# Four graph layers on one core: the first pairs of the second layer ahead of the first layer's last sums, with checks, constants and turned factors in another order

## The chip, the core and the metric

The kernel runs on one core of a Trainium2 chip. The core has five instruction queues: TensorE (PE, matrix products, with its weight loads as PEld), VectorE (DVE), ScalarE (ACT), GpSimd (POOL) and SyncE (SP, which here only issues loads and stores). Each works through its own instructions in the order in which they were put down; between engines they wait for one another on semaphores. Data lie in SBUF; PE writes to PSUM[...]. The metric is the device time of one execution in microseconds, the median of several runs. A profile of one further execution shows where the time goes.

## The reference

Four layers run over one graph of 4096 nodes with 64 features each. `adj` is a dense 4096 by 4096 matrix of zeros and ones in float32, 64 MB, and every layer needs all of it. After each layer comes `x = layernorm(x + layer(x))`. Cut to what matters:

```python
# layer 0: mean over neighbours
deg = clip(sum(adj, 1) + 1, 1);  h = (adj @ x + x) / deg
z = relu(concat([x, h], 1) @ W + b);  out = z / max(norm(z), 1e-12)
# layers 1 and 3: attention in hyperbolic space, over all pairs (i, j)
left, right = logmap0(x) @ w_l, logmap0(x) @ w_r
a = sigmoid(left[:, None] + right[None, :] + b) * adj
out = proj(expmap(x, einsum('ij,ijd->id', a, logmap(x[:, None], x[None, :]))))
# layer 2: the last 100 neighbours, weights halving from the end of the row
w = mask * where(pos > 0, 0.5 ** (k - pos), 0);  out = w @ (x @ weight) + bias
```

## The kernel before

**Tiles and stages.** The 4096 nodes are cut into four groups of 1024 (`s`), worked through as 3, 2, 1, 0 (`GROUPS`). For a group, the matrix comes in 16 loads of 1 MB (`load`, L706): load `g`, from 15 down to 0, holds blocks `2g+1` and `2g` of 128 source nodes by the group's 1024 target nodes. So each layer takes 64 loads; I count them through, load 0 to 63 in layer 0, so that load `16n + 15 - g` is load `g` of the n-th group. All come through SP, into six buffers (`f_loads`): a load is issued when all readers of the one six before it are done.

**Layer 0** (L1556 to 1613). Each load gets eight products on PE (L1571): the features as a high and a middle part (`first`) and as a low part with a column of ones (`third`), which gives sums and degrees in four PSUM banks of a group (`acc`, six banks in all). DVE checks for each of the 256 parts of the matrix that it holds zeros and ones only (`check`, L869, one instruction of 128x2048). `checked_later` (L712) puts half of the checks of every group into layer 2, where the same part is loaded again; in layer 0 the checks of `g` = 15, 14, 13, 12, 10, 8, 6 and 4 are done. At a group's end ACT copies the four banks to SBUF, and the *row work* of the group follows: `end_0` (L1507: products with the weights at L1519 and L1520, division by the degree, relu, norm), `norm_rows`, and `prepare` (L950), whose second half (`second`, L970) makes the group's factors for the pairs. Four of them are turned (transposed on PE at L1025, copied on ACT at L1029): `hi_lo` and `src`, with which the group enters the pairs as sources, and `lo_hi` and `dst`, with which it enters as targets, and which are needed only when its own 1024 targets have their turn. For the last group of the order much of that runs on POOL instead of DVE (`pooled`). `constants` (L1478) spreads the biases over the partitions and makes the columns of the attention weights.

**Layers 1 and 3** (`attend`, L1118). For each target group, each of 16 loads makes two half steps: six products into a tile `z` of two banks (L1152, 1155, 1158), `sig` and `sq` on ACT (L1170, L1173), `t = max(z, 0) * sig` on DVE (L1176); and for both halves together `t = (sq + c) * t` on DVE (L1179) and eight products into the sum `acc` (L1130), two loads later. `need((layer, 2 * g // WB))` asks for the source group's factors before the first load that uses them: the last group's at the 13th load.

**Layer 2** (`wide_pass`, `narrow_pass`) counts neighbours with products at L1756, takes powers on ACT (L1763) and adds up at L1722 and L1768. `supports` (L1398) makes `x @ weight` of a group from rows: `x_hl` on ACT and POOL (L1403, L1404), turned on PE (L1409), multiplied (L1419).

**Order.** Row work is written as generators that `yield` a number of ticks. `later` puts one into one of two queues; `tick` (L617) is called some times for each load and runs what is due; `need` ticks until something is done. `take` (L677) hands out the PSUM bank for row work (`aux`), and every second time a spare one while there is one; `spare_ends` ticks until none is in use. In layers 0 and 2 the order of PE and ACT is that of the program text (`FIXED`); else the scheduler places instructions. `anchored`, where set, puts row work of PE, ACT and DVE behind the pair work (or checks) that stands before it in the text.

**The border from layer 0 to layer 1.** After its last load the last group's four banks are copied by ACT, `end_0` is queued, and `need((0, s, "rows"))` runs it up to its division, then `spare_ends`. Only then `attention` begins.

## Time and profile before

| what | time |
|---|---|
| median of 3 runs | 1062.61 us (1061.79 to 1067.7) |
| the profiled execution | 1063.81 us |
| its span in the profile | 1062.1 us |
| mean granted PE clock | 0.975 of full |
| layer 0, to the last copy of its sums | 0 to 184.1 us |
| layer 1, first to last target group | 188 to 515 us |
| layer 2 | 515 to 716 us |
| layer 3 and the end | 715 to 1062 us |

The stages are read from the first and last instructions of L1571, L1152 and L1756 in the timeline. The profile's page gives busy time by engine and in 40 slices of 26.6 us; the trace behind it can be asked for the timeline of one engine, for waits, for the chain of work that ended last, and for busy time in chosen stretches. In a timeline row stand the start, the duration, the engine, the line, what is written from what, the count, and in brackets the idle time before it and what ended that.

### The profile page before, as it was taken

Reading aid. Unit: us, or ns where it says so; the run is one execution under the profiler, and the core shown is the slowest. Engines: PE = TensorE matmul, PEld = TensorE weight load, DVE = VectorE, ACT = ScalarE, POOL = GpSimd, SP = SyncE. Lnnn points to the kernel's source line nnn. Section 1 sums busy time; section 2 is a strip of 40 time slices with the busy share of each in tenths; the row PEclk is TensorE's granted clock in tenths of the full one; section 3 lists DMA queues with packets and bytes.
Section 4 is the critical chain, followed back from the end, with each engine's and each line's share of the span. In section 5 each row is a group of like instructions: output and inputs, shape, how many; then the busy total and the mean of one; then the engine's idle time right before and its main releaser. Section 6 shows DMA issues by size and latency. Waiting matters only on the chain.

```text
span 1062.1 us, 13509 instructions
## 1 busy us (share of the span) xinstructions
PE 981.6 (92%) x4760; PEld 401.9 (38%) x4845; DVE 900.2 (85%) x1383; ACT 753.1 (71%) x876; POOL 339.0 (32%) x695
## 2 busy tenths in 40 slices
PE   5998998889999999999999999999899999999991
PEld 2454554333333333333333344543333333333330
DVE  7577877788999999999475579858899999999996
ACT  0013122779989888898667688897898888888870
POOL 0011212480155365365210020104401562573660
PEclk8899999899999999999999999999999999999996
DMA  9999999755665666567589999996465765665600
GB/s 357 359 418 368 394 390 387 300 180 176 238 208 207 220 238 207 189 238 238 204 300 336 371 366 304 327 333 233 143 218 194 243 232 204 242 207 203 234 1 23
DMA packets 38580, 271.62 MB, mean 256 GB/s; under 512 B 4710, under 2 KB 4710, under 8 KB 5734
## 3 DMA queue, kind: packets, MB, share of 16 engines
q1 hardware_dynamic: 37728, 270.03, 69.6%
q8 instruction: 40, 0.66, 0.2%
q10 hardware_dynamic: 774, 0.63, 0.2%
q14 instruction: 38, 0.31, 0.1%
HBM read 269.58 MB, written 1.05 MB: 255 GB/s over the span
## 4 chain that ended last, share of the span: by engine, by line
PE 62%; DVE 21%; ACT 6%; POOL 6%; issue 2%; DMA 2%; ACTq 0%; SPq 0%; POOLq 0%; DVEq 0%
PE acc L1130 16%; PE z L1756 11%; PE z L1155 7%; PE z L1158 7%; PE z L1152 7%; DVE t L1179 6%; DVE t L1176 6%; PE acc L1571 5%; PE z L1768 3%; DVE junk L871 2%; PE z L1722 2%; DMA edges<-in_adj_dram 2%; ACT sq L1173 2%; ACT sq L1763 1%; POOL sq L1535 1%
## 5 line engine op out<-in xcount | busy, mean ns | idle before, releaser
L1176 DVE SCALAR_TENSOR_TENSOR t<-z,sig 128x1024 f32<-128x1024 f32 x256 | 309.1, 1219 | 22.4 <-ACT sq L1173 20.1
L1173 ACT ACTIVATE sq<-z 128x1024 f32<-128x1024 f32 x256 | 255.1, 1022 | 59.1 <-PE z L1158 29.2
L1179 DVE SCALAR_TENSOR_TENSOR t<-sq,t 128x2048 f32<-128x2048 f32 x127 | 293.3, 2309 | 0.3
L1170 ACT ACTIVATE sig<-left_b,right 128x1024 f32<-128x1024 f32 x256 | 286.6, 1149 | 3.6 <-DVE t L1176 3.2
L1130 PE MATMUL acc<-t,xe 128*64 128x512 f32 x1024 | 259.8, 611 | 7.9 <-DVE t L1179 7.0
L1155 PE MATMUL z<-lo_hi,hi_lo 128*128 128x512 f16 x512 | 194.4, 380 | 3.8 <-issue 1.1
L1158 PE MATMUL z<-dst,src 74*128 74x512 f16 x512 | 195.4, 382 | 0.0
L1152 PE MATMUL z<-edges,two_i 128*128 128x512 bf16 x463 | 181.8, 393 | 5.8 <-DVE t L1176 5.8
L1763 ACT ACTIVATE sq<-z 128x512 bf16<-128x512 f32 (+1 forms) x192 | 137.9, 741 | 43.0 <-PE z L1756 41.2
L1130 PEld LDWEIGHTS acc<-t,xe 128*64 128x64 f32 x1024 | 64.2, 137 | 137.2 <-issue 109.8
L871 DVE SCALAR_TENSOR_TENSOR t<-edges 128x2048 bf16<-128x2048 f32 x32 | 73.3, 2300 | 28.7 <-DMA edges<-in_adj_dram 28.5
L1152 PEld LDWEIGHTS <-two_i 128*128 128x128 bf16 x512 | 50.3, 98 | 124.7 <-issue 74.3
L1571 PE MATMUL acc<-edges,first 128*128 128x512 bf16 x241 | 77.9, 400 | 16.8 <-DMA edges<-in_adj_dram 16.3
L1756 PE MATMUL z<-edges,pass_by 128*128 128x512 bf16 x241 | 85.2, 390 | 6.8 <-ACT sq L1763 5.8
L1756 PE MATMUL z<-edges,enter 128*128 128x512 bf16 x248 | 86.3, 388 | 0.4
L871 DVE SCALAR_TENSOR_TENSOR junk<-edges 128x2048 bf16<-128x2048 f32 x32 | 73.1, 2284 | 15.7 <-DMA edges<-in_adj_dram 15.7
L1571 PE MATMUL acc<-edges,third 128*65 128x512 bf16 x256 | 81.1, 398 | 0.8 <-issue 0.2
L1158 PEld LDWEIGHTS <-src 74*128 74x128 f16 x512 | 49.3, 96 | 73.0 <-issue 11.6
L1155 PEld LDWEIGHTS <-hi_lo 128*128 128x128 f16 x512 | 50.4, 98 | 58.3 <-issue 12.8
L1279 POOL TENSOR_TENSOR w_att<-x,u 128x512 f32<-128x512 f32 x6 | 18.1, 3022 | 163.5 <-ACT u L1273 163.5
L1722 PE MATMUL z<-sq,halves 128*128 128x512 bf16 x122 | 45.9, 377 | 0.8 <-ACT sq L1763 0.6
L1535 POOL TENSOR_TENSOR sq<-z 128x512 f32<-128x512 f32 x4 | 10.1, 2524 | 114.2 <-DVE z L1533 94.6
(466 smaller groups left out, 1002.3 us busy)
## 6 DMA issues: line engine op xcount, KB each, us to landing
edges<-in_adj_dram SPq DMA_DIRECT2D x256, 1024.0 KB, 4.9
x<-in_x_dram SPq DMA_DIRECT2D x4, 256.0 KB
out_dram<-x ACTq DMA_DIRECT2D x2, 256.0 KB
out_dram<-x SPq DMA_DIRECT2D x2, 256.0 KB
w_sb<-in_L_gnn_W_dram ACTq DMA_DIRECT2D x1, 32.0 KB, 5.3
w_twice<-in_L_gnn_weight_dram ACTq DMA_DIRECT2D x2, 16.0 KB, 4.6
given<-in_L_gnn_b_dram ACTq DMA_DIRECT2D x1, 0.2 KB
given<-in_L_gnn_bias_dram ACTq DMA_DIRECT2D x1, 0.2 KB
```

The lines of the kernel that those rows point to most:

```text
L871: V.scalar_tensor_tensor(junk, a, 0.0, a, ALU.not_equal, ALU.not_equal, accum_out=odd[:, n : n + 1])
L1130: it = nc.tensor.matmul(acc[h * D : (h + 1) * D, :], xe[:, j, :], t[:, k, h * W : (h + 1) * W], start=j == BLOCKS[0], stop=j == BLOCKS[-1],)
L1152: nc.tensor.matmul(half, two_i, edge[:, at : at + W], start=True, stop=False)
L1155: nc.tensor.matmul(half, hi_lo[:, of], lo_hi[:, to], start=False, stop=False)
L1158: last = nc.tensor.matmul(half, src[:, of], dst[:, to], start=False, stop=True)
L1170: nc.scalar.activation(sig, left_b, AF.Sigmoid, bias=right[:, j : j + 1])
L1173: nc.scalar.activation(sq[:, k], zp, AF.Square, bias=ROOT + OFF, scale=-1.0 / UNIT)
L1176: V.scalar_tensor_tensor(ts[k][:, k], zp, 0.0, sig, ALU.max, ALU.mult)
L1179: V.scalar_tensor_tensor(t, sq, HIGH**2, t, ALU.add, ALU.mult)
L1571: nc.tensor.matmul(accs[h][:m], lhs[:, j, :], edge[:, at : at + W], start=j == BLOCKS[0], stop=j == BLOCKS[-1],)
L1756: nc.tensor.matmul(z[:, h : h + W], lhs, rhs[:, h : h + W], start=j == BLOCKS[0], stop=True, skip_group_check=True,)
L1763: weighed[0] = nc.scalar.activation(w, z[:, :n], AF.Exp, bias=-(OFF_EDGE + CUT) * LN2, scale=-LN2)
```

## The change

1. The checks of `g` = 6 and 4 of groups 3 and 2 move from layer 0 to layer 2.
2. `constants` becomes a generator in the queue, with waits of some ticks between its parts; `att_columns` is cut into the products (`att_products`) and the rest. The first group's `linear` follows behind it in the same queue entry.
3. In layer 0, row work is anchored from the second group on.
4. In layers 1 and 3, group 1 is treated as group 0 in that `lo_hi` and `dst` are turned last, after the group counts as ready (`late`). In layer 1's preparation, group 1 takes its two logarithms as a series on DVE (`half_log_of_ratio`) instead of on ACT.
5. At the end of layer 0 ACT loads the sigmoid's table by an activation of one element; half of the four copies goes to DVE; and `end_0` of the last group is not run there. `attention` queues it, to begin 4 ticks into the pairs, with `attend`'s own bank `acc` as the spare bank until the first products of L1130 need it.
6. `supports` waits 4 ticks instead of 2 for `x_hl` in layer 2.

```diff
             def checked_later(s, g):
-                return g in (0, 1, 2, 3, 5, 7, 9, 11)
+                return g in (0, 1, 2, 3, 5, 7, 9, 11) or (s in GROUPS[:2] and g in (4, 6))
...
-                    by_log = layer == 3 and s != GROUPS[-1]
+                    by_log = s != GROUPS[-1] and (layer == 3 or s == GROUPS[-2])
...
-                    for parts in turns[:2] if pooled else turns:
+                    late = s in GROUPS[2:]
+                    for parts in turns[:2] if late else turns:
                         yield from turn(*parts)
...
                     done.add((layer, s))
-                    if pooled:
+                    if late:
                         for parts in turns[2:]:
                             yield from turn(*parts)
...
                 acc = ps.tile([P, W], F32, name="acc")
+                if layer == 1 and s == GROUPS[0]:
+                    spare.append(lambda dtype, shape: of_bank(acc, dtype, shape))
...
                             if len(lag) == 2:
+                                if spare:
+                                    spare_ends()
                                 add_up(*lag.pop(0), last)
...
-                yield 2
+                yield 4 if place[0] == 2 else 2
...
                     t = aux.tile([P, 2 * D + 3], F32, name="aux")
                     nc.tensor.matmul(t, one_row, given, start=True, stop=True)
+                    yield 4
                     V.tensor_copy(given_b, t)
+                    yield 8
...
-                    return (
-                        curved(c1, "k1", 1e-15**0.5), curved(c3, "k3", 1e-15),
-                        att_columns(att_rows1, "att1"), att_columns(att_rows3, "att3"),
-                    )
+                    made.append(curved(c1, "k1", 1e-15**0.5))
+                    made.append(curved(c3, "k3", 1e-15))
+                    for rows_of, name in ((att_rows1, "att1"), (att_rows3, "att3")):
+                        w = att_products(rows_of)
+                        yield 8
+                        made.append(att_columns(w, name))
+                    yield 4
...
                     for s in GROUPS:
+                        anchored[0] = s != GROUPS[0]
...
-                                curve1, curve3, att1, att3 = constants()
...
-                                later(in_turn((0, s), linear(0, s, w0_sb[:D, :], own_part)))
+                                own_of = linear(0, s, w0_sb[:D, :], own_part)
+                                later(in_turn((0, s), constants(), own_of))
                             tick(4)
                         need((0, s))
+                        curve1, curve3, att1, att3 = made
+                        last = s == GROUPS[-1]
+                        if last:
+                            nc.scalar.activation(turned_on, one_row[:, :1], AF.Sigmoid)
                         tops = []
                         for h in range(2):
                             top = row.tile([P, W], F32, name="sums", bufs=2)
-                            nc.scalar.copy(top, sums[h])
+                            copy = V.tensor_copy if last and h else nc.scalar.copy
+                            copy(top, sums[h])
...
-                            nc.scalar.copy(low, counts[h][: D + 1])
+                            copy(low, counts[h][: D + 1])
                             tops.append((top, low))
-                        later(end_0(s, tops))
-                        if s == GROUPS[-1]:
-                            need((0, s, "rows"))
+                        if not last:
+                            later(end_0(s, tops))
...
                     anchored[0] = n > 0
                     then = GROUPS[n + 1] if n + 1 < NW else None
+                    if n == 0 and layer == 1:
+                        later(end_0(GROUPS[-1], tops), False, 4)
                     sums = attend(layer, s, rates[n], then)
```

`of_bank` is the old `of_third` of layer 2, made general: it gives a PSUM bank the shape that is asked for.

More of the change, by code (lines that the diff above doesn't have):

```diff
@@ L684, in take, with of_bank @@
                 return spare[0](dtype, shape)
+            def of_bank(t, dtype, shape):
+                if dtype == F16:
+                    return t.bitcast(F16)
+                n = int(np.prod(shape[1:]))
+                if len(shape) == 2:
+                    return t[:, :n]
+                names = "abc"[: len(shape) - 1]
+                return t[:, :n].rearrange(
+                    "p (%s) -> p %s" % (" ".join(names), " ".join(names)),
+                    **dict(zip(names, shape[1:])),
+                )
             def spare_ends():
@@ L848, in att_rows, with att_products @@
                 return t
-            def att_columns(rows_of, name):
+            def att_products(rows_of):
                 t = aux.tile([P, 2], F32, name="aux")
@@ L858, in att_columns @@
                     )
+                return t
+            def att_columns(t, name):
                 w = row.tile([P, 2], F32, name="att_w")
@@ L1531, in end_0 @@
                     held.clear()
-                    done.add((0, s, "rows"))
                     V.tensor_scalar(z, z, 0.0, None, ALU.max)
@@ L1553, in end_0 @@
                     )
+                made = []
+                turned_on = keep.tile([1, 1], F32, name="turned_on")
                 with tc.manual_schedule(engines=FIXED):
                     for s in GROUPS:
+                        anchored[0] = s != GROUPS[0]
                         sums = [ps.tile([P, W], F32, name="acc") for _ in range(2)]
@@ L1613, in stream @@
                 spare_ends()
+                anchored[0] = False
             place[0] = 1
@@ L1777, in stream @@
             row_bank = ps.tile([P, W], F32, name="acc")
-            def of_third(dtype, shape):
-                t = row_bank
-                if dtype == F16:
-                    return t.bitcast(F16)
-                n = int(np.prod(shape[1:]))
-                if len(shape) == 2:
-                    return t[:, :n]
-                names = "abc"[: len(shape) - 1]
-                return t[:, :n].rearrange(
-                    "p (%s) -> p %s" % (" ".join(names), " ".join(names)),
-                    **dict(zip(names, shape[1:])),
-                )
             with tc.manual_schedule(engines=FIXED):
-                spare.append(of_third)
+                spare.append(lambda dtype, shape: of_bank(row_bank, dtype, shape))
                 for some in (GROUPS[:2], GROUPS[2:3], GROUPS[3:]):
```

## The prediction

> **What bounds the kernel now.** First I read the page for the engines as a whole: the busy rows and the slices.
>
> ```profile
> PE 981.6 (92%) x4760; PEld 401.9 (38%) x4845; DVE 900.2 (85%) x1383; ACT 753.1 (71%) x876; POOL 339.0 (32%) x695
> ...
> DVE  7577877788999999999475579858899999999996
> ...
> DMA  9999999755665666567589999996465765665600
> ```
>
> The averages hide three regimes. In layer 0 (seven slices) the DMA row is at 9 and DVE is not: the loads decide. In the attention slices DVE is at 9 and DMA at 5 or 6: there each load costs DVE two L1176 and one L1179, 2 x 1.15 + 2.2 = 4.5 us from start to start. The change touches the loads of layer 0, the border to layer 1, one wait in layer 2 and the border to layer 3; the middle of the pairs stays as it is.
>
> Second, does layer 0 load at full speed? I added the trace's DMA packets up to loads of 1 MB and took each load's last packet. Loads 16 to 27 land 2.51 us apart (53.24 to 80.86); that is full speed. Longer gaps stand at loads 8 to 12 (29.31 to 43.34: 14.0 for four), 29 and 31 (3.57 and 4.17), 45 and 47 (3.84 and 4.18), 63 (3.91). The chain of waits has three of them, the last right behind a check of DVE:
>
> ```profile
> 90.30 7.08 DMA edges<-in_adj_dram
> ...
> 133.86 6.91 DMA edges<-in_adj_dram
> ...
> 173.09 2.22 DVE junk L871 x2
> 175.36 5.34 DMA edges<-in_adj_dram
> ```
>
> So buffers come free too late, and SP's own waits say who frees them: checks first (103.6 us), PE second.
>
> ```profile
> SPq L708 <- DVE junk L871: 103.6, 28, 6.3
> SPq L708 <- PE acc L1571: 37.7, 27, 7.5
> ```
>
> Third, the timeline of PE in the first group. PE stands for `given_b`, which DVE copies only behind two checks; load 3 had landed at 15.3, its products start at 24.7, and SP issues load 9, into its buffer, at 28.34.
>
> ```profile
> 16.22 0.49 PE L1481 MATMUL aux<-given,one_row 1*128 1x131 f32 x2
> 21.04 1.01 PE L855 MATMUL aux<-one_row,xw 1*128 1x1 f32 x4 [4.33 <-DVE given_b L1482]
> 22.30 1.01 PE L855 MATMUL aux<-one_row,xw 1*128 1x1 f32 x4 [0.25 <-DVE att_w L860]
> ```
>
> Fourth, the border to layer 1: DVE stands for the last sums, then for POOL, and PE with it.
>
> ```profile
> 185.00 0.18 DVE L1525 RECIPROCAL deg<-aux 128x4 f32<-128x4 f32 x1 [4.70 <-PE aux L1520]
> ...
> 191.64 1.22 DVE L1176 SCALAR_TENSOR_TENSOR t<-z,sig 128x1024 f32<-128x1024 f32 x1 [0.32 <-ACT sq L1173]
> 196.68 0.69 DVE L924 TENSOR_REDUCE n_m<-z 128x8 f32<-128x512 f32 x1 [3.82 <-POOL z L1542]
> ```
>
> Fifth, layer 2, where PE is the bound (9.4 to 9.9 of 10 us busy, but 7.79 from 540 to 550):
>
> ```profile
> 543.76 0.62 PE L1409 MATMUL aux<-ident,x_hl 128*128 128x128 f16 x8 [2.14 <-DVE un L756]
> 544.21 0.61 PE L1756 MATMUL z<-edges,pass_by 128*128 128x512 bf16 x2
> 544.66 0.78 PE L1756 MATMUL z<-edges,enter 128*128 128x512 bf16 x2
> 545.37 1.92 PE L1768 MATMUL z<-sq,halves 128*64 128x512 bf16 x8
> ```
>
> The name in the bracket is only the last signal; DVE's `un` is not read here. POOL's L1404 makes `x_hl` from 540.42 to 543.70.
>
> **The change, part by part.** Sums are made against the profiled run, 1063.81 us (span 1062.1); it lies 1.2 us above the median of the runs, so the forecast is the gain taken off the median.
>
> *Constants in steps.* In the new order PE does three loads between the product for `given` and the first `att` products, and two more before the second. DVE's order up to the fourth check is the same: that check ends at 20.8, so load 9 can be issued then, long before load 8's packets end. Four gaps fall from 14.0 to 10.0: **-4.0**. The small steps of the attention columns only change places among rows of 0.15 us; the parts of `first` for groups 2, 1 and 0 come near 16, 25 and 37, before loads 4, 8 and 12 land (17.8, 29.3, 39).
>
> *Four checks fewer.* They take 4 x 2.29 = 9.2 us from DVE in layer 0. On the path is only load 31, issued at 89.88 when the check begun at 87.52 ended: 4.17 - 2.5 = **-1.7**. Load 29 waits for `g` = 8, which stays behind the norm's row work (80.59): its 1.1 stays. In layer 2 the same 9.2 us fall between 563 and 582, where DVE waits for loads (4.7, 2.3 and 4.4 us idle before the next piece); PE holds such a buffer some 9 us longer than the check would, so nothing. Without that cover: 9.2.
>
> *Anchored order.* In groups 1 and 0 DVE's new order has the checks of `g` = 6 and 4 ahead of two 0.69 us steps and some eight small ones. The gap at load 47 falls from 1.7 to 0.5 over 2.5, that at 63 from 1.4 to 0.1; load 45 still waits for `g` = 8 and loses 0.3: about **-2.4**. Sum for the loads: the last one of layer 0 lands at 179.6 - 8.1 = 171.5, and its products end near 174.6.
>
> *The end of layer 0.* Here DVE is late next. Load 48 lands 6.6 earlier, at 133.4, and DVE has just then ended group 2's row work, so the checks of group 0 begin at 134.0 instead of 140.87; 25 us to `g` = 8 as before (140.87 to 165.88), 2.3 for it, 3.3 for ten small and two large row steps, 4.6 for two checks: 169.5. Behind them now stands group 1's second half: 5.5 us of old steps, the logarithm's 17 new ones at 0.1 to 0.2 (3.2), three to `f` (0.6), then two copies (0.6 each, 0.55 apart): 179.9. What the logarithm takes away is two 0.2 us activations and a 0.36 us wait, so it costs 3 us of DVE. PE's queue holds the sums of the half that DVE copies *ahead* of the first pairs: all pairs stand behind DVE. PE idles 175.4 to 180.0, then 2.1 us of sums and 1.3 of pairs at full clock, 1.1 for `sq`: first L1176 at 184.5. Here a rule bears. The Trainium skill (TensorE: Matmul & The Clock Gate, Part 1) has PE at half clock after an idle window of some 3.4 us and for as long after. The row: after 3.56 us idle at 198.67 pair products ran 0.42 apart, not 0.22. So 3.0 + 2.6 + 1.1: 186.8. But at 543.76 a wait of only 2.14 was enough: L1768's eight took 1.92, not 1.05. I take the cold value, by these rows; both ends stay. Before it was 191.64. The early table load costs nothing: in the old run its 1.28 (at 185.03) lay in ACT's wait for PE too.
>
> *The last group's row work among the pairs.* I compare at the end of the 12th L1179, 261.87 before. From 191.64 that is 70.2 us: 24 x 1.15 + 12 x 2.2 = 54.0 of pairs, 6.2 row work, 10.0 idle (3.82, 2.22, 0.75, 1.57, 1.35, 0.25). After: row work 6.2 - 1.0 (group 1's last steps) + 3.2 (division to norm, once before the pairs) = 8.4; idle 1.5 at the start, 3.0 for POOL's first root (5.3 against two L1176), 1.2 at the variance, 1.4 at the reciprocal, 2.0 at the logarithm's activation: 9.1. So 186.8 + 71.5 = 258.3 cold, 255 or so warm: 3.6 to 6.9, I take **-4.0**. It is half of what the loads gain.
>
> *`supports` two ticks later*: one half step, 2.9 us; PE then arrives at 544.2, POOL is done at 543.70. The wait of 2.14 goes, and with it the slow products: steps from 539.55 to 545.37 and on to 550.12 took 10.6 where 2.9 each plus 0.45 and 0.7 for the turns make 7.0. By the rule above 2.14 us is too short an idle to cool, so -2.1; by the row -3.6. I take **-3.3**. Group 1's `halves` come under 1 us later (L1426 at 551.76 before) and are needed from 555.7 on, group 0's 2.9 later than 576.9, needed near 583.
>
> *Right factors of group 1 last.* In layer 2's last pass each ACT copy of 0.9 lengthened its step by 0.63 (starts 1.99 instead of 1.36 apart); two go: -1.3. In the pairs of layer 3 they meet a DVE that is full from 719 to 732; ACT has room but for the first steps. Bounds 0 and -2.5 (with the chain of group 0 earlier); **-1.2**, near the row.
>
> Sum: -4.0 - 3.3 - 1.2 = **-8.5**: 1055.3 for the profiled run, 1054.1 on the median.
>
> **Rivals.** *The loads' gain comes through whole.* If DVE is done by 175.5 (its pieces in layer 0 are 0.08 apart where independent, 0.2 where not; I took the middle) the pairs start at 180 to 182: 8 + 3.3 + 1.2 = 12.5, 1050. Against it: the new steps are a chain. *The border takes everything.* If DVE is 4 later than 179.9, only 4.5 is left: 1058. For it: the gain in the loads counts for nothing once DVE is last. *Slower: the chain of group 0 comes too late for the 13th load.* Place: POOL's steps among L1179. The Trainium skill (SBUF — State Buffer, Who interferes with whom) says DVE and POOL exclude each other on a shared port for a whole instruction; here POOL steps that began in an L1179 took 2.17 to 2.35 instead of 0.20, seven of them before 250 (14 us of a chain of 65). By the rows' order I count one block less at the first root and one less at the second; by the rule any step that meets an L1179 blocks. Ten more blocks are 20 us: the chain ends near 277 instead of 257, the 13th load waits, and of the border's -4 a +15 is left, less 4.5 from the later layers: 1073. The change loses from four or five more blocks on (8.5 over 2). Against it: two of the covers in the new order are L1176 alone, which reads PSUM.
>
> **How the numbers follow.** Forecast 0.57 (own range 1050 to 1058), whole gain 0.16, border takes all 0.18, slower 0.09. The range 1047 to 1062 leaves out the slower case and the ends of the others. A difference of 0.5% (5.3 us) is what a measurement of this kernel can tell from none: below 1057.3 is faster. The forecast gives 0.53 of its chance to that and the whole gain all of it: 0.69. The border case and a rest of the forecast make 0.22, slower 0.09.
>
> **What would show it.** Load 12 landing near 39 and load 63 near 171 to 173; no wait over 1 us at the `att` products; DVE's copies of the last sums ending near 180 with PE idle before them; the 12th L1179 of layer 1 ending 3 to 7 us earlier; no wait at L1409 near 540. I am wrong if layer 0's loads still show gaps of 4 us at loads 9 and 10, if the 13th load waits for its factors, or if layer 2's loads are issued behind checks.

## The result and the profile after

The changed kernel takes **1050.22 us** (median of 4 runs, 1049.27 to 1051.42) where the kernel before takes 1062.99 (1061.79 to 1067.7): a ratio of 0.9865, 95% interval 0.9833 to 0.9898. The profiled execution took 1051.42 us with a span of 1049.7. On a second chip (the sixth experiment) the ratio was 0.9894, 0.987 to 0.9919, from 1062.87 to 1050.42.

The page of the changed kernel, engines first and then slices:

```profile
PE 977.7 (93%) x4845; PEld 397.9 (38%) x4845; DVE 907.8 (86%) x1401; ACT 751.7 (72%) x873; POOL 322.1 (31%) x695
...
DVE  7486978789999999999488579858999999999996
...
DMA  8999999655665566566599998996465666665600
```

The busy times hardly moved. What moved are the waits. SP's own show that layer 0 now loads better: it waited 10.5 us less for checks and 4.9 less for PE than before (103.6 and 37.7).

```profile
SPq L720 <- DVE junk L886: 93.1, 26, 6.4
SPq L720 <- PE acc L1598: 32.8, 23, 2.4
```

The lines have shifted: a check is L886, the pairs' steps on DVE are L1196 and L1199, the sums of layer 0 L1544 and L1545, the turned products of `supports` L1429. (In some of the experiments they lie a few lines off.) The page counts the checks too: 32 in layer 0 and 32 in layer 2 before, 28 and 36 now. That is 64 in all, one of 128x2048 for each load of 1 MB, and not 256 as the description of the kernel has it.

At the end of layer 0, DVE's timeline shows its two copies, then eight small steps of row work up to 181.2, then nothing until the first pair:

```profile
179.02 0.68 DVE L1636 COPY u<-acc 65x512 f32<-65x512 f32 x1
179.62 0.68 DVE L1628 COPY sums<-acc 128x512 f32<-128x512 f32 x1
...
187.56 1.23 DVE L1196 SCALAR_TENSOR_TENSOR t<-z,sig 128x1024 f32<-128x1024 f32 x1 [6.33 <-ACT sq L1193]
```

PE's timeline tells why. It stood 4.11 us for DVE. The bracket names `own` (L1070), the last reader of the PSUM bank that the sums go to; it ends 0.2 us behind the copies, which stand ahead of it in DVE's order. The products behind the wait run 0.43 us apart, at half clock, until 187.06; from 187.43 on they are 0.22 apart:

```profile
180.63 0.66 PE L1544 MATMUL aux<-sum_w,sums 128*128 128x65 f32 x2 [4.11 <-DVE own L1070]
181.09 0.64 PE L1545 MATMUL aux<-count_w,u 65*128 65x65 f32 x2
...
187.06 0.53 PE L1176 MATMUL z<-dst,src 74*128 74x512 f16 x1
187.43 0.39 PE L1170 MATMUL z<-edges,two_i 128*128 128x512 bf16 x1
```

Along the span the two first profiles differ like this (us, end of the step unless said):

| point | before | after | shift |
|---|---|---|---|
| load 12 lands | 43.34 | 40.47 | -2.9 |
| load 31 lands | 94.18 | 89.10 | -5.1 |
| load 63 lands | 179.62 | 173.06 | -6.6 |
| first pair step on DVE starts | 191.64 | 187.56 | -4.1 |
| 12th L1179 / L1199 of layer 1 | 261.96 | 257.26 | -4.7 |
| 64th of layer 1 | 512.62 | 507.78 | -4.8 |
| wide pass, 64th exponential | 610.51 | 601.95 | -8.6 |
| last exponential of layer 2 | 715.05 | 705.63 | -9.4 |
| 12th L1179 / L1199 of layer 3 | 789.81 | 777.07 | -12.7 |
| end of the span | 1062.08 | 1049.68 | -12.4 |

So the loads gave 6.6, the border to layer 1 took 1.8 of it back, the wide pass gave 3.8, the border to layer 3 gave 4.1.

### The profile page after: what moved, and what is told of

Its sections match the earlier page's. It is cut to its first block, busy times and chain, and to the rows that moved or that the text cites. A ratio compares the mean times of both kernels' runs of the same rounds, so it can differ in the third digit from the quotient of the medians.

```text
span 1049.7 us, 13606 instructions
## 1 busy us (share of the span) xinstructions
PE 977.7 (93%) x4845; PEld 397.9 (38%) x4845; DVE 907.8 (86%) x1401; ACT 751.7 (72%) x873; POOL 322.1 (31%) x695
## 4 chain that ended last, share of the span: by engine, by line
PE 60%; DVE 22%; DMA 6%; POOL 5%; ACT 4%; issue 2%; ACTq 0%; SPq 0%; POOLq 0%; DVEq 0%
PE acc L1148 16%; PE z L1790 11%; PE z L1170 8%; DVE t L1199 7%; PE z L1176 7%; PE z L1173 7%; DVE t L1196 6%; DMA edges<-in_adj_dram 5%; PE z L1802 3%; DVE junk L886 3%; PE acc L1598 3%; PE z L1756 2%; ACT sq L1193 2%; ACT sq L1797 1%; DMA w_twice<-in_L_gnn_weight_dram 1%
## 5 line engine op out<-in xcount | busy, mean ns | idle before, releaser
L1196 DVE SCALAR_TENSOR_TENSOR t<-z,sig 128x1024 f32<-128x1024 f32 x256 | 308.6, 1218 | 24.9 <-ACT sq L1193 22.7
L1199 DVE SCALAR_TENSOR_TENSOR t<-sq,t 128x2048 f32<-128x2048 f32 x127 | 294.5, 2319 | 0.3
L1148 PE MATMUL acc<-t,xe 128*64 128x512 f32 x1024 | 255.7, 605 | 16.0 <-DVE t L1199 14.7
L1170 PE MATMUL z<-edges,two_i 128*128 128x512 bf16 x512 | 201.1, 393 | 1.1 <-DVE t L1196 1.1
L886 DVE SCALAR_TENSOR_TENSOR t<-edges 128x2048 bf16<-128x2048 f32 x36 | 82.4, 2304 | 19.7 <-DMA edges<-in_adj_dram 19.5
L1598 PE MATMUL acc<-edges,first 128*128 128x512 bf16 x256 | 80.2, 394 | 20.5 <-DMA edges<-in_adj_dram 20.0
L1170 PEld LDWEIGHTS <-two_i 128*128 128x128 bf16 x512 | 50.4, 98 | 119.9 <-issue 74.7
L1176 PEld LDWEIGHTS <-src 74*128 74x128 f16 x512 | 49.2, 96 | 72.6 <-issue 10.6
L886 DVE SCALAR_TENSOR_TENSOR junk<-edges 128x2048 bf16<-128x2048 f32 x28 | 64.0, 2284 | 11.7 <-DMA edges<-in_adj_dram 11.6
L1299 POOL TENSOR_TENSOR w_att<-x,u 128x512 f32<-128x512 f32 x6 | 16.2, 2707 | 149.5 <-ACT u L1293 149.5
L1756 PE MATMUL z<-sq,halves 128*128 128x512 bf16 x128 | 48.0, 377 | 0.2 <-ACT sq L1797 0.2
L1404 ACT COPY x_t<-aux 64x512 f32<-64x512 f32 x8 | 4.6, 576 | 57.5 <-PE aux L1399 57.5
```

Of the source, the lines that this page charges most:

```text
L886: V.scalar_tensor_tensor(junk, a, 0.0, a, ALU.not_equal, ALU.not_equal, accum_out=odd[:, n : n + 1])
L1148: it = nc.tensor.matmul(acc[h * D : (h + 1) * D, :], xe[:, j, :], t[:, k, h * W : (h + 1) * W], start=j == BLOCKS[0], stop=j == BLOCKS[-1],)
L1170: nc.tensor.matmul(half, two_i, edge[:, at : at + W], start=True, stop=False)
L1176: last = nc.tensor.matmul(half, src[:, of], dst[:, to], start=False, stop=True)
L1196: V.scalar_tensor_tensor(ts[k][:, k], zp, 0.0, sig, ALU.max, ALU.mult)
L1199: V.scalar_tensor_tensor(t, sq, HIGH**2, t, ALU.add, ALU.mult)
```

## Experiments

Twelve kernels ran, each with a profile and timed in five rounds against the kernel before. Since single executions start layer 0 differently, I compare stages and not spans (landings are good to some 0.3 us): when load 63 lands, how long after it the 32nd L1179 (or L1199) of layer 1 ends, how long the wide pass takes from first to 64th exponential (the powers on ACT, L1763), and how long it is from there to the 12th L1179 of layer 3.

| kernel | load 63 lands | to the 32nd L1179 | wide pass | to layer 3's 12th | ratio to before, interval |
|---|---|---|---|---|---|
| before, first profile | 179.62 | 178.81 | 99.95 | 179.30 | |
| before, again (5) | 182.21 | 178.16 | 96.49 | 177.83 | 1.0, 0.9983 to 1.0018 |
| `supports` alone (1) | 177.32 | 177.91 | 96.08 | 179.19 | 0.9982, 0.9963 to 1.0 |
| right factors alone (2) | 180.91 | 178.48 | 96.49 | 174.82 | 0.9961, 0.9938 to 0.9984 |
| order of the logarithm alone (3) | 182.26 | 179.61 | 96.47 | 175.39 | 0.9967, 0.9952 to 0.9983 |
| changed, first profile | 173.06 | 180.44 | 96.23 | 175.12 | 0.9865, 0.9833 to 0.9898 |
| changed, again (6) | 171.59 | 180.38 | 96.25 | 175.25 | 0.9894, 0.987 to 0.9919 |
| sums 8 ticks in (4) | 171.67 | 181.77 | 96.23 | 175.10 | 0.9921, 0.9897 to 0.9945 |
| copies on ACT (7) | 172.32 | 176.19 | 96.24 | 174.79 | 0.9864, 0.984 to 0.9887 |
| more checks moved (8) | 170.86 | 174.79 | 96.25 | 176.58 | 0.987, 0.9843 to 0.9897 |
| constants at once (9) | 173.60 | 180.04 | 96.24 | 175.13 | 0.9918, 0.9892 to 0.9945 |
| logarithm on ACT (10) | 171.78 | 176.29 | 96.23 | 175.12 | 0.9863, 0.9831 to 0.9894 |
| group 0's checks moved (11) | 172.22 | 174.73 | 96.24 | 175.13 | 0.9858, 0.9828 to 0.9888 |
| sums before the pairs (12) | 169.87 | 177.89 | 96.24 | 175.13 | 0.9852, 0.9826 to 0.9878 |

Runs 1 to 4 shared one chip, 5 to 8 another, 9 to 11 and 12 had theirs. A ratio carries the scatter of the kernel before, whose executions lie between 1055 and 1070 us; so the intervals of kernels that differ by 3 to 5 us overlap. Where I say below that one variant of the changed kernel is faster than another, it rests on the stages and on the times themselves: the changed kernel took 1048.86 to 1052.44 in its ten executions.

### 1. `supports` alone

```diff
-                yield 2
+                yield 4 if place[0] == 2 else 2
```

> The kernel before with one edit: supports waits 4 ticks for x_hl in layer 2 instead of 2. In the changed kernel the wide pass of layer 2 ended 8.6 us earlier while it had begun 4.8 earlier, so 3.7 to 3.8 us were gained between, against 3.3 forecast. Theory of the cold clock (the row at 543.76: a wait of 2.14 us was enough to halve the clock): alone the edit gives -3.3 to -3.8 us, 1059 to 1059.7 on a median of 1063, PE has no wait over 0.5 us at L1409 and the eight L1768 behind it take about 1.05 us instead of 1.92. Rival, the rule of 3.4 us: the clock's dip at 540 to 550 has another cause and stays; the wait alone goes, -2.1. Third: the 2.1 us gained are given back because the supports of group 1 come later; no change.

Measured: no wait at the turned products (541.18), the clock at 1.00 from 540 to 550, and a wide pass of 96.08 instead of 99.95. But the ratio to the kernel before is 0.9982 (0.9963 to 1.0): 1.9 us, anything from 0 to 3.9. The next two kernels have the old `supports` and a wide pass of 96.5. The gain of 3.9 us against the first profile is real for that execution, and not what the edit is worth in every one; the fifth run explains it.

### 2. Right factors of group 1 last, alone

```diff
-                    for parts in turns[:2] if pooled else turns:
+                    late = pooled or (layer == 3 and s == GROUPS[2])
+                    for parts in turns[:2] if late else turns:
...
-                    if pooled:
+                    if late:
```

> The kernel before with one edit: in layer 3 the right factors of group 1 are turned after the group counts as ready. The changed kernel gained 4.2 us between the last step of layer 2 and the 12th L1199 of layer 3, where 1.2 were forecast. Theory: the copies themselves give 2 us at the border and cost 2.2 in the first pairs of layer 3; the gain is that the scheduler now puts the logarithm of group 0 (with its table load) behind two sq of the pairs, where it stood ahead of them and held ACT 3.0 us for POOL. Then this edit alone gives -4 us (about 1059), and DVE's four waits between 759 and 772 (1.85, 1.72, 1.27, 1.56) shrink to 2 us in sum. Rival: the 4.2 need the other edits (the checks moved into layer 2, the earlier start); alone it gives -1.2 and the four waits stay.

Measured: the border to layer 3 is 4.5 us shorter than in the first profile, 3.0 shorter than in the second of the kernel before. Layer 2's end gives 1.2, the step from there to the first pair 1.0, and the pairs to the 12th L1179 take 68.04 instead of 70.39 (68.87 in the second profile), although two copies have come to lie among them. The edit needs none of the others. The median is 1058.99 us, the ratio stands for 4.1 us (1.7 to 6.6).

### 3. Only the order of the logarithm

```diff
-                        nc.scalar.activation(t, t, AF.Ln, bias=1.0)
-                        nc.scalar.activation(q1, q1, AF.Ln, bias=1.0, scale=-1.0)
+                        for it in (
+                            nc.scalar.activation(t, t, AF.Ln, bias=1.0),
+                            nc.scalar.activation(q1, q1, AF.Ln, bias=1.0, scale=-1.0),
+                        ):
+                            if layer == 3:
+                                behind_pairs(it.ins)
```

`behind_pairs` ties an instruction behind the last pair work on its engine.

> The kernel before with only the order on ACT changed: in layer 3 the two logarithms of group 0 are tied behind the pair work that precedes them in the text, which puts one sig and one sq ahead of the table load; no right factor is moved. Theory of the order: DVE's waits between 759 and 772 (6.4 us) fall to 3 to 4, -2 to -3.5 us (1059.5 to 1061). Rival, that the moved copies bring the gain: no change to -0.5, or slower by up to 1 because the logarithm comes 2 us later and the factor of the 13th load with it.

Measured: 66.47 us from the first pair step to the 12th L1179, 3.9 less than in the first profile and 2.4 less than in the second, with the right factors where they were. In ACT's timeline of the kernel before, the table load stands directly behind the copy of `hi_lo`, and ACT then waits for POOL with the pairs' `sq` queued behind:

```profile
752.57 1.02 ACT L1029 COPY hi_lo<-aux 128x1024 f16<-128x1024 f16 x1
753.60 1.28 ACT L1036 ACT_TABLE_LOAD   x1
757.91 0.21 ACT L1036 ACTIVATE tt<-tt 128x8 f32<-128x8 f32 x1 [3.02 <-POOL tt L1007]
758.02 1.01 ACT L1173 ACTIVATE sq<-z 128x1024 f32<-128x1024 f32 x1
```

In this kernel one `sig` and one `sq` stand ahead of it, and the wait is 1.07:

```profile
753.45 1.17 ACT L1183 ACTIVATE sig<-left_b,right 128x1024 f32<-128x1024 f32 x1
754.50 1.03 ACT L1186 ACTIVATE sq<-z 128x1024 f32<-128x1024 f32 x1
755.55 1.28 ACT L1046 ACT_TABLE_LOAD   x1
757.90 0.21 ACT L1046 ACTIVATE tt<-tt 128x8 f32<-128x8 f32 x1 [1.07 <-POOL tt L1016]
```

DVE's four waits between 759 and 772 fall from 6.4 us to 2.5. The changed kernel has two `sq` ahead of the table load, and no wait behind it:

```profile
746.28 1.97 ACT L1193 ACTIVATE sq<-z 128x1024 f32<-128x1024 f32 x2
748.26 1.28 ACT L1052 ACT_TABLE_LOAD   x1
749.69 0.21 ACT L1052 ACTIVATE tt<-tt 128x8 f32<-128x8 f32 x1
```

So has run 2, where nothing but the moved turns can have brought it about. Most of the gain at this border, then, is an order on ACT that the edit did not ask for; the moved copies give 2 us before the pairs and cost 1.6 among them (68.04 against 66.47).

### 4. The sums 8 ticks into the pairs

```diff
-                        later(end_0(GROUPS[-1], tops), False, 4)
+                        later(end_0(GROUPS[-1], tops), False, 8)
```

> The changed kernel with one number changed: the last group's sums of layer 0 begin 8 ticks into the pairs instead of 4, which puts the first products of the pairs ahead of them on PE. Theory that PE's place behind DVE's copies costs the border: the wait of 4.11 us at 180.63 and the slow clock behind it go, the first L1196 starts near 181.5 instead of 187.56, and 3 to 5 us of that are left at the 12th L1199 (257.3 to 253 or so): 1045.5 to 1047. Rival, that the chain of group 0's row work sets the 12th load: its products come some 2 us later, what is gained at the start is lost in waits of DVE for POOL in the first twelve loads, and the time is 1050 to 1052.

Measured: the pairs do start at once, at 182.15, and PE keeps the full clock. Against the first profile of the changed kernel 2.7 us of the 5.4 are left at the 12th L1199, 0.8 at the 16th, nothing at the 32nd. Counted from load 63 the 32nd comes 1.4 later, and the kernel is slower: 1053.51 us. Four of DVE's waits show where the gain went. The first two were shorter in the changed kernel, the other two were not there. First the changed kernel, then this one:

```profile
211.00 0.69 DVE L939 TENSOR_REDUCE n_m<-z 128x8 f32<-128x512 f32 x1 [2.26 <-POOL z L1566]
...
227.44 0.20 DVE L977 RECIPROCAL rb<-b 128x8 f32<-128x8 f32 x1 [1.37 <-POOL b L974]
```

```profile
210.00 0.69 DVE L939 TENSOR_REDUCE n_m<-z 128x8 f32<-128x512 f32 x1 [4.00 <-POOL z L1566]
...
228.25 0.20 DVE L977 RECIPROCAL rb<-b 128x8 f32<-128x8 f32 x1 [2.22 <-POOL b L974]
...
237.21 0.23 DVE L1064 TENSOR_SCALAR m<-b,k_of_y 128x8 f32<-128x8 f32 x1 [1.62 <-POOL xe L1012]
...
257.60 2.35 DVE L1196 SCALAR_TENSOR_TENSOR t<-z,sig 128x1024 f32<-128x1024 f32 x2 [2.33 <-ACT sig L1190]
```

The rival holds for the first loads: DVE stands for the last group's row work on POOL, which begins with the sums. It is not the whole account. The last wait is for ACT, and POOL's chain does not end later: its last step (L1023) starts at 242.93, in run 6 at 244.63, with load 63 at the same time. What makes the 32nd come later than in run 6 stays open.

### 5 and 6. Both kernels again

> The kernel before, unchanged, for a second profile. In the first one POOL's x_hl (L1404) began at 540.42, 0.02 us after a check on DVE, and took 3.28 us; in two kernels with the same layer 2 (the late right factors, the order of the logarithm) it began before the check, took 1.18 and 1.16, PE's wait was 1.1 instead of 2.14, and the wide pass was 3.5 us shorter (96.5 instead of 99.95 from first to 64th exponential). Theory: that collision depends on when a load lands and is not in every execution; a second profile of the kernel before has a wide pass of 96.5 and the later wait of 1.1 about as often as not. Rival: those two kernels differ from the kernel before in something that reaches layer 2; then this profile shows 99.95 again.

> The changed kernel, unchanged, beside the kernel before on one chip, for a ratio and as the base of the two runs that follow. First measurement: 0.9865, interval 0.9833 to 0.9898. If the wide pass of the kernel before is usually as short as in the two other kernels, the ratio is nearer 0.99 (3.5 us less gain than between the two profiles: 9 us); if not, 0.9865 again.

In the first profile of the kernel before, POOL's `x_hl` and a check on DVE collide. POOL began 0.02 us behind the check and took 3.28 us (start, duration, from the timelines of DVE and POOL):

```profile
540.40 2.29 DVE L871 SCALAR_TENSOR_TENSOR t<-edges 128x2048 bf16<-128x2048 f32 x1 [0.76 <-DMA edges<-in_adj_dram]
540.42 3.28 POOL L1404 TENSOR_TENSOR x_hl<-x,x_hl 128x512 f16<-128x512 f32 x1 [30.22 <-ACT x_hl L1403]
```

In the second profile it began 0.01 us *ahead* of the check, took 1.16, and the check on DVE took the long time (3.28 instead of 2.29):

```profile
542.52 3.28 DVE L871 SCALAR_TENSOR_TENSOR t<-edges 128x2048 bf16<-128x2048 f32 x1 [0.81 <-DMA edges<-in_adj_dram]
542.51 1.16 POOL L1404 TENSOR_TENSOR x_hl<-x,x_hl 128x512 f16<-128x512 f32 x1 [30.23 <-ACT x_hl L1403]
```

PE starts the turned products at 543.72 with no wait that its timeline shows and keeps its clock, and the wide pass is 96.49. Of four profiles with the old `supports` three have POOL at 1.16 to 1.18 us and a wide pass of 96.5 (the wait of 1.1 us that the expectation speaks of lies elsewhere: it is a sum over two waits of the weight loads). With the new `supports` POOL is blocked in three of ten profiles, both of the changed kernel (3.16 us from 535.62, and 3.13) and run 9 (3.23). Each time PE's turned products come 0.7 to 0.8 us behind POOL's end, and the wide pass is 96.23 to 96.25: two ticks later PE no longer comes in time to wait. So the edit saves 0.3 us where the two don't collide and 3.7 where they do. How often they would collide in the changed kernel without it, no run shows.

Side by side with the second profile of the kernel before, the changed one gains 10.6 at load 63, gives 2.2 back at the border, and gains 0.2 in the wide pass and 2.6 at the border to layer 3: 11.2 of the 11.4 us between the spans.

### 7. All four copies on ACT

```diff
-                            copy = V.tensor_copy if last and h else nc.scalar.copy
+                            copy = nc.scalar.copy
```

> The changed kernel with all four copies of layer 0's last sums on ACT. In the changed kernel DVE's two copies end at 180.2, behind all of its row work of group 1, and PE's first sums start at 180.63. ACT is done with its own two at 177.6. Theory of the forecast (DVE is last at the end of layer 0 and PE stands behind it): the four are done at 178.6, PE starts 2 us earlier, and so does all that follows, the chain of the last group's row work among it: first L1196 near 185.5, and -2 still at the 12th and 16th L1199 (255.3 and 275.8): ratio to the changed kernel 0.998. Rival: two more copies and src ahead of sig and sq make ACT the late one: 0 to -0.5 at the 16th.

Measured: PE waits 1.87 us instead of 4.00 (run 6), its products stay 0.22 apart, the first L1196 starts 2.2 us earlier than in run 6 although load 63 landed 0.7 later, and from load 63 to the 32nd L1199 it is 4.2 us less. Twice what I expected: the half clock, in which run 6 spends 6.8 us here, goes too. The medians differ by 3.2 us (1047.19 and 1050.42).

```profile
178.63 0.41 PE L1544 MATMUL aux<-sum_w,sums 128*128 128x65 f32 x2 [1.87 <-DVE own L1070]
```

### 8. The checks of groups 1 and 0 moved too

```diff
-                return g in (0, 1, 2, 3, 5, 7, 9, 11) or (s in GROUPS[:2] and g in (4, 6))
+                return g in (0, 1, 2, 3, 5, 7, 9, 11) or g in (4, 6)
```

> The changed kernel with the checks of g = 6 and 4 of groups 1 and 0 moved to layer 2 too (nothing is left out). Theory of the forecast: with DVE last at the end of layer 0, 4.6 us fewer of it there bring its copies from 180.2 to about 177 (then the last product of PE, 176, is what they wait for), PE waits 1 us instead of 4.1 and stays at full clock: first L1196 at 182 to 183 instead of 187.56, and 4 us or so of that at the 12th and 16th L1199, because the sums themselves come earlier; loads 45, 61 and 63 may gain 1 more. In layer 2 the four checks cost nothing where DVE waits for loads: 1045 to 1047. Rival: in layer 2, at the end of group 0, DVE's row work is on the path to layer 3, and 2 to 5 us are given back there: 1048 to 1051.

Measured: DVE's copies now wait 2.3 us for PE's last products, PE waits 1.0, and the stretch to the 32nd L1199 is 5.6 us shorter. Layer 2 gives 1.3 back, all between the 119th and the 127th exponential, in group 1. The median is 1047.79 us.

### 9. Constants in one go again

```diff
                     nc.tensor.matmul(t, one_row, given, start=True, stop=True)
-                    yield 4
                     V.tensor_copy(given_b, t)
-                    yield 8
...
                         w = att_products(rows_of)
-                        yield 8
                         made.append(att_columns(w, name))
```

> The changed kernel with the waits inside constants taken out again (the products and copies in one go, as before). Load 12 should land 3 to 5 us later (43.5 to 46 instead of 40.5). In the changed kernel DVE waited 3.2 us for load 48 at 132.8 and then had 2.4 us of waits in all until its copies ended at 180.2. Theory, that the loads' gain passes through to the border because DVE's last stretch begins with a landing: first L1196, 12th and 16th L1199 and the end 3 to 5 us later than in the changed kernel, 1053.5 to 1055.5. Rival, that DVE is last at the border by its own amount of work and the loads' gain counts for nothing there: 0 to 1 us, 1050 to 1051.5.

Measured: PE's wait at the `att` products is back, loads 8 to 12 take 12.1 us instead of 10.3, load 63 lands at 173.60, 2.0 later than in run 6. The median is 1052.64 us.

```profile
22.78 1.01 PE L866 MATMUL aux<-one_row,xw 1*128 1x1 f32 x4 [5.80 <-DVE given_b L1502]
```

From load 63 to the 32nd L1199 it is the same 180 us. So what loads gain or lose passes through to layer 1 whole, and the rival falls. At load 63 the edit shows as 0.5 to 2.0 us against the two profiles of the changed kernel, because the first loads start differently. Counted from the landing of load 3 it is plain: to load 12 it takes 26.2 us here, and 24.0 to 24.3 in the other eight profiles of the changed kernel and its variants. That is 2 us for the waits inside `constants`, less than the 3 to 5 I expected.

### 10. Group 1's logarithms on ACT again

```diff
-                    by_log = s != GROUPS[-1] and (layer == 3 or s == GROUPS[-2])
+                    by_log = layer == 3 and s != GROUPS[-1]
```

> The changed kernel with group 1's two logarithms of layer 1 on ACT again, as before the change. It takes 17 steps off DVE, 3.2 us by the forecast, against two activations of 0.2 and a wait of 0.36. Theory (DVE is last, PE stands behind its copies): the copies end at 177 to 177.5, PE waits 1 to 1.5 instead of 4.1 and keeps the full clock: first L1196 at 182.5 to 184, and -2.5 to -4 at the 16th L1199: 1046.5 to 1048. Rival: ACT's logarithm waits for DVE and stands ahead of the copy of hi_lo and the load of the sigmoid's table on ACT's queue; then ACT's copies and sig come later by what DVE saves: 1049.5 to 1051, or later.

Measured: DVE waits 0.36 us for ACT's logarithm, then 1.56 for PE's last products; PE waits 1.02 instead of 4.00. To the 32nd L1199 it is 4.1 us less. This part of the change makes the kernel slower: with it undone the median is 1045.98 us, four executions of five below all of the changed kernel's.

### 11. Only group 0's checks moved

```diff
-(s in GROUPS[:2] and g in (4, 6))
+(s != GROUPS[2] and g in (4, 6))
```

> The changed kernel with the checks of g = 6 and 4 of group 0 moved to layer 2, those of group 1 left in layer 0. When both groups' were moved, the narrow pass of layer 2 lost 1.33 us in group 1 (between the 119th and the 127th exponential) and nothing in group 0. Theory: at the end of layer 0 the same 4.6 us of DVE go as there, so the first L1196 comes within 1.5 us of 180.2 and the 16th L1199 within 1.5 of 270, and layer 2 loses nothing: 1044.5 to 1047, at or under the run with both. Rival: group 1's two checks in layer 0 hold loads 45 and 47 and push all of DVE's work for group 0 back, so that half of the gain goes: 1047.5 to 1049.

Measured: PE waits 1.02 us, it is 5.7 us less to the 32nd L1199, as with both groups' checks, and nothing lost in layer 2 (175.13). The median is 1045.76 us (1044.64 to 1047.42), below every execution of the changed kernel, though on another chip. The ratios alone can't tell the two apart: 0.9858 here, 0.9865 and 0.9894 there.

```profile
177.32 0.41 PE L1544 MATMUL aux<-sum_w,sums 128*128 128x65 f32 x2 [1.02 <-DVE own L1070]
```

### 12. The sums ahead of the pairs, as before the change

```diff
-                        if not last:
-                            later(end_0(s, tops))
+                        later(end_0(s, tops))
+                        if last:
+                            need((0, s, "rows"))
...
-                    if n == 0 and layer == 1:
-                        later(end_0(GROUPS[-1], tops), False, 4)
```

`attend`'s bank is not lent out either, and `end_0` reports `rows` again behind the division.

> The changed kernel with the last group's sums of layer 0 ahead of the first pairs again, as before the change; all the rest of the change stays. Theory, that this part of the change is worth something by itself: DVE's copies still end near 178 to 180, the sums, the division and the norm then stand between them and the pairs, so the first L1196 comes 4 to 6 us later than in the changed kernel (190 to 193) and the 12th and 16th L1199 2 to 4 us later, 1052.5 to 1054.5. Rival, from the run in which the pairs were put further ahead and nothing was left of 5.4 us at the 16th: what sets the first 16 loads is the chain of the last group's row work on POOL, which begins with the sums; with the sums first it begins no later, so the pairs start later but wait less, and the 16th L1199 moves by less than 1 us: 1049.5 to 1051.5.

Measured: against both expectations, faster. 1046.98 us (0.9852) and 2.5 us less from load 63 to the 32nd L1199. The first pair starts at 184.66, 14.8 us behind load 63, where the changed kernel needs 13.7 to 14.5: the sums ahead of it cost at most 1.1 us. PE's timeline says how:

```profile
175.28 0.44 PE L1542 MATMUL aux<-sum_w,sums 128*128 128x65 f32 x2 [0.82 <-ACT sums L1628]
...
178.26 0.41 PE L1542 MATMUL aux<-sum_w,sums 128*128 128x65 f32 x2
178.49 0.61 PE L1543 MATMUL aux<-count_w,u 65*128 65x65 f32 x2
```

PE begins with the half that *ACT* has copied, and waits 0.82 us; by the time it comes to DVE's half, DVE is done. In the changed kernel DVE's half comes first and the pairs stand behind it, while ACT's half, ready at 177.6, stands behind the pairs. From the start of the first pair step to the end of the 16th L1179 (or its successor) the kernels compare as follows (DVE, us: time in which a pair step runs, time in which only row steps run, and the rest):

| | pairs | row steps | idle | in all |
|---|---|---|---|---|
| before | 74.8 | 4.6 | 10.4 | 89.9 |
| changed, again (6) | 75.4 | 6.3 | 9.3 | 91.0 |
| sums before the pairs (12) | 74.7 | 4.7 | 7.1 | 86.5 |

Of the 4.5 us between the last two rows, 1.6 are the row steps that cost nothing where DVE waits for PE anyhow; 2.2 are waits and 0.7 longer pair steps. POOL's chain begins earlier too: its last step, for the last group's factor, starts at 228.86 instead of 244.63. Whether the place of the sums brings this or the order of the two halves, no run separates.

## Why the prediction was right, and where it was not

**The sum.** 8.5 us were forecast on 1062.61, so 1054.1; 12.8 came (12.5 on the second chip). The time lies inside the stated range, and the mechanism was right where it counts: the loads gain 8, DVE is last at the end of layer 0, and part of the gain is given back there. Three terms were mis-sized. 12.5 is also the number of the rival in which the loads' gain comes through whole, but that rival was not what happened: DVE was not done by 175.5, and the pairs started at 187.56, not at 180 to 182. That the numbers meet is luck. (Runs 8 and 11 do bring the pairs to 180.17 and 181.53.)

**Loads: right in size.** -8.1 was forecast at load 63. The first pair of profiles shows -6.6. Over five profiles with the old layer 0 load 63 lands at 180.5 on average (177.3 to 182.3), over four of the changed kernel or with its layer 0 unchanged up to the last copies (6, 4, 7 and the first) at 172.2 (171.6 to 173.1): -8.3. Load 12 was to land near 39 and did at 40.2 to 40.8. The four gaps I looked at are 10.3 us instead of 14.0, but loads 1 to 8 come no earlier (30.13, before 29.31). The same five profiles and four divide the 8.3 by stretches. Load 3 lands alike (16.2 and 16.3 on average), so it isn't luck with the first loads. From load 3 to load 12 it takes 27.8 us on average before (26.2 to 29.3) and 24.2 after: 3.6, for which 4.0 was forecast for the constants; run 9 shows 2 of it in the waits inside them. From load 12 to load 63 it takes 136.6 and 131.7: 4.9, where the fewer checks and the anchored order were to give 4.1. No run undoes either of these two alone. The moved checks cost layer 2 nothing, as forecast: its wide pass is 96.23, and 96.08 with the new `supports` alone.

**The end of layer 0: right.** DVE is last, its copies end at 180.3 (forecast 179.9), PE stood 4.1 us and the first L1196 came at 187.56 (forecast 186.8 cold). That the times agree so well is in part luck: load 63 had landed 1.6 later than forecast. Counted from it, the copies end 7.2 and 7.3 us later in the two profiles (forecast 8.4) and the first pair starts 14.5 and 13.7 later (forecast 15.3). Four runs take something off that point and all move the whole of layer 1: copies on ACT, fewer checks twice, the logarithm. The logarithm was priced at 3 us of DVE; undone it gives 4.1; the half clock goes with it.

**Row work among the pairs: right in kind, half the size, and a loss.** The border was to give back 4.1 of 8.1. At the 12th L1199, where the forecast was made, it gives back 2.1 on average (84.2 behind load 63 against 82.1), at the 32nd 1.8 (180.4 against 178.6). The forecast saw that row work goes up (by 2.2; the timeline has 1.7) and the wait of DVE for POOL (3.0 forecast, 2.26 and 2.08 measured). What it didn't ask is whether the sums would have cost anything in their old place. Run 12 answers: at most 1.1 us. The move that names the change takes 2.5 us more than it gives.

**`supports`: mis-sized.** -3.3 was read from one collision of POOL with DVE in one execution. There it is right (3.7). In three of four profiles of the old code the wait is not there, and the edit is worth 0.3. Run 1 gives 1.9 us over many executions, between 0 and 3.9. Where the wait is gone the clock from 540 to 550 is 1.00 (run 1, and the second profile of the kernel before).

**Right factors of group 1: mis-sized.** -1.2 was forecast from two copies leaving layer 2; the border gained 2.6 to 4.2. The copies leave layer 2 as was said, for 1.2 us. The step that failed is "ACT has room but for the first steps": it took the order on ACT as given. The logarithm's table load ahead of the pairs' `sq` was in the profile, with its wait of 3.02, and I had not looked at whether the edit would move it.

**The slower rival did not come.** Five POOL steps were blocked for about 2 us each before 250 in the changed kernel, seven before. (Of the seven, five are small steps of 0.2 us; two are steps of 128x512 that took 3.02 and 2.79 where others of that shape take 1.0 to 1.2.) Its place was right, though: once the pairs start earlier, DVE waits longer for POOL and most of the gain goes there (run 4).

Taken together: the forecast was 4 us short because the border gave back 2 us less than it said and the factors gave 2.4 more; `supports` at -3.3 was too much and hid a part. In averages over the profiles it is -8.3 for the loads, +1.8 for the border, -1.1 for `supports` and -3.6 for the border to layer 3 (175.2 against 178.8): -11.2. The last 1.3 to 1.6 us of the measured gain are not accounted for; single executions of the kernel before scatter by more than that.

Not tried: run 12's order together with the checks of run 11 or the logarithm of run 10; the changed kernel with its two halves of sums exchanged, with the old `supports`, or without the anchored order; and how the loads would go with DVE's copies shared out in another way.

## What to carry to other kernels

A step in front of the bottleneck's first instruction is nearly free as long as the bottleneck waits there for something else; moved behind it, it costs its length, and more where other work waits for it. So before work is moved off a border, read what the busiest engine is waiting for there, and which half of the work is ready first. And take a wait from more than one profile before pricing it: one that hangs on two engines starting within 0.02 us of each other is there in some executions only, and a scheduler's order that no edit mentions can be worth more than the edit.

## What the runs showed of the hardware

When POOL and DVE met at `x_hl`, the one that began second bore the whole delay: POOL 3.28 us instead of 1.16 when 0.02 late, DVE 3.28 instead of 2.29 when 0.01 late.

The half clock didn't follow the length of PE's wait. Behind 4.11 us it began at once and lasted to 187.35; behind 4.00 us (run 6) the products ran 0.22 apart for 0.9 us, then at half clock to 186.96; behind 1.87 (run 7) it did not come. In run 12 it came at 178.50 and lasted to 185.33, with no wait of PE over 0.82 us in the 20 us before. And in layer 3 the two profiles of the kernel before wait alike on PE (2.90 and 2.88 us at L1041, to 762.53 and 761.20), yet the granted clock from 760 to 770 is 0.83 in the first and 1.00 in the second: 1.5 us of the border to layer 3 hang on that.

The profiles' own record of the granted clock shows more than I read from the waits. In all fourteen, each stretch at half clock but the last, which runs into the end, is a whole number of windows of 3.41 us (one to four), and they lie on one grid within a profile: in the first, 186.56, 196.80, 544.96 and 763.41 are whole multiples of 3.413 us apart. Where a wait lies on that grid goes with what follows. Of the 2.90 us above, 2.53 fall into the window from 760.00, PE is busy for 0.88 of its 3.41, and the next window is at half clock. In the second profile a border at 759.65 cuts the 2.88 into 1.33 and 1.55, and the clock stays. Busy PE is no safeguard either. In run 12, and in the kernel before, PE works nearly all of the window ahead of the half clock, but on nothing except the f32 sums (behind the stretch and its length stand the busy times of PE, PEld, DVE, ACT and POOL, then the granted PE clock):

```profile
183.15:186.56 3.41, 3.31 (x30) 3.17 (x29) 1.03 (x3) 3.38 (x5) 0.00 (x0) 1.00 0.99 408
186.56:189.97 3.41, 3.19 (x17) 2.15 (x18) 1.46 (x4) 2.59 (x3) 0.82 (x1) 0.50 1.00 423
```

```profile
175.09:178.50 3.41, 3.18 (x27) 3.04 (x27) 2.86 (x12) 3.41 (x5) 0.00 (x0) 1.00 1.01 428
178.50:185.33 6.83, 6.20 (x33) 3.71 (x33) 4.79 (x17) 2.96 (x4) 1.87 (x6) 0.50 0.91 380
```

Runs 2, 6 and 10 have such a window too (from 184.09, 53.84 and 53.02), each with half clock behind it. So the rule that I weighed in the prediction, an idle window of some 3.4 us, fits these runs in the window and not in the idle; and the wait of 2.14 us at 543.76 lay whole in one window, from 541.55, in which PE was busy for 1.27 of 3.41 us. How much work of which kind keeps the clock, and for how many windows it then stays low, is open.
